# Routed experts of a GNN and MoE stack: visiting each expert once, in one of twelve ways by its count of rows

## The chip, the cores and the metric

The kernel runs on one core of one Trainium2 chip. The metric is device microseconds of one execution. The profile is a recording of one execution by the hardware profiler, and its span is the time from the first to the last recorded instruction.

## The reference

The state `x` has 625 rows (nodes) of 512 float32 features. Four layers follow each other, and each adds a graph part and then a feed-forward part to `x`, both of them on a layer norm of it. Layers 0 and 2 have feed-forward parts with eight small experts that see every row. The change concerns layers 1 and 3, where each row goes to two of eight large experts:

```python
# layer 1: 512 -> 1024 -> 512
logits = x @ gate_w + gate_b                      # 625 x 8
topk_vals, topk_idx = top_k(logits, 2); w = softmax(topk_vals)
h = relu(x @ w1[e] + b1[e]);  y_e = h @ w2[e] + b2[e];  out = sum_e w_e * y_e
# layer 3: 512 -> 1536 -> 512
probs = softmax(x @ router_w.T); gates, idx = top_k(probs, 2); gates /= sum(gates)
h = silu(x @ w1[e].T) * (x @ wgate[e].T);  y_e = h @ w2[e].T;  out = sum_e gate_e * y_e
```

So 1250 pairs of row and expert are computed in each of the two layers. The reference's router, on its inputs, gives the eight experts these counts of rows: in layer 1 they are 96, 346, 175, 23, 54, 50, 350 and 156; in layer 3 they are 197, 240, 352, 99, 77, 43, 149 and 93.

## The kernel before

The kernel is one program for all layers. A scheduler puts each instruction on its engine's queue in the order of the source, as far as the data allow, and sets semaphores between the engines. All matmuls of the experts are float32, and each shows in the trace as two matmul instructions, each with its weight load.

Weights lie in HBM as chunks of 128 partitions by 2048 float32 (1024 KB): an expert of layer 1 has 4 chunks (2 up, 2 down), one of layer 3 has 9 (6 up in 3 pairs of `w1` and `wgate`, 3 down). `routed` keeps a ring of 11 chunks. `refill` issues the next load on SyncE's queue as soon as a chunk has been read.

`dispatch` (L514) turns the router's choice into blocks of B = 128 rows. It ranks the rows of each expert with small matmuls (`ps_rk`), works out how many blocks each expert has beyond its first, gives each pair a place in one of NB = 17 blocks, and builds with one-hot matmuls (`ps_id`) the row numbers `node` and the weights `gate` of every block. Blocks 0 to 7 are the first blocks of the eight experts. Blocks 8 to 16 are overflow blocks; `own` names the expert of each of them.

`routed` (L619) then computes block by block. For each block:

- `fetch(b)` gathers 128 rows from HBM (an indirect DMA that GpSimd issues), two blocks ahead.
- `enter(b)` (L671) turns them with four TensorE transposes (`ps_x`) and copies them to `xgT`.
- `ahead(b, c)` multiplies the rows with an up chunk (`ps_h`, L1170 in layer 1, L1335 in layer 3): the 128 rows are the stationary side, 512 columns of weights are moved.
- `turn(b, c)` (L685) turns the hidden values (`ps_t`).
- `back(b, c)` (L692) multiplies them with a down chunk (`ps_y`, L697) and, after the last chunk, scales by `gate` (VectorE, L703) and adds the rows into `sums` in HBM (an indirect DMA that GpSimd issues, L705).

The first eight blocks are one straight list of units. The overflow blocks stand one inside the other in conditional blocks:

```python
def overflow(i):
    if i < NO:
        with tc.If(n_over > i):
            run([(E + i, c) for c in range(nch)], i + 1 < NO)
            overflow(i + 1)
```

Every engine executes each of these branches itself (L730 in the profile). The counts need 14 blocks in layer 1 (six of them overflow) and 13 in layer 3 (five overflow); an expert's weights are loaded again for each of its blocks.

In layer 1, `expert_bias` (matmuls `ps_eb`) and `normalise` (25 steps on VectorE and one on ScalarE, for the adjacency matrix of layers 2 and 3) are run as `fill` between the units of the first blocks.

Of the kernel before, what the change touches and what calls it, by code (L numbers as in the profile page):

```python
# [20 lines left out]
NT = 5  # L21
# [20 lines left out]

B = 128
NB = 17
NO = NB - E
# [31 lines left out]
def _weights(i):  # L77
# [15 lines left out]
    for e in range(E):  # L93
        a, g = _chunks(i["L3_ffn_w1"][e].T), _chunks(i["L3_ffn_wgate"][e].T)
        for c in range(3):
            w += [a[c], g[c]]
        w += _chunks(i["L3_ffn_w2"][e].T)
# [55 lines left out]
def kernel(  # L153
# [360 lines left out]
    def dispatch(layer, o12, weight, w0, per):  # L514


        with tc.tile_pool(name=f"{layer}d", bufs=1) as dp:
# [4 lines left out]
            rank, tot = ps[:T, 0, :NT * E], ps[:, 1, :E]  # L522
            nc.tensor.matmul(rank, tri, mask.rearrange("p t e -> p (t e)"), start=True, stop=False,
# [6 lines left out]
            for s in range(NT):  # L530
                nc.tensor.matmul(tot, ones16, mask[:, s, :], start=(s == 0), stop=(s == NT - 1))
            gt = dp.tile([P, E, 4], F32, tag="gt", name="gt")
            nc.vector.tensor_tensor(gt, tot[:, :, None].to_broadcast([P, E, 4]),
                                    thr[:, None, :].to_broadcast([P, E, 4]), op=OP.is_gt)
            nov = dp.tile([P, E], F32, tag="nov", name="nov")
            nc.vector.tensor_reduce(nov, gt, axis=AX.X, op=OP.add)
            pm = dp.tile([P, E, E], F32, tag="pm", name="pm")
            nc.vector.tensor_mul(pm, before, nov[:, None, :].to_broadcast([P, E, E]))
            ovb = dp.tile([P, E], F32, tag="ovb", name="ovb")
            nc.vector.tensor_reduce(ovb, pm, axis=AX.X, op=OP.add)  # L540
            delta = dp.tile([P, E], F32, tag="delta", name="delta")
            nc.vector.scalar_tensor_tensor(delta, ovb, float(B), dconst, op0=OP.mult, op1=OP.add)
            rk = rank.rearrange("p (t e) -> p t e", e=E)
            sl = dp.tile([T, NT, E], F32, tag="sl", name="sl")
            nc.vector.scalar_tensor_tensor(sl, rk, float(B),
                                           delta[:T, None, :].to_broadcast([T, NT, E]),
                                           op0=OP.is_ge, op1=OP.mult)
            nc.vector.tensor_add(sl, sl, rk)
            nc.vector.tensor_add(sl, sl, e128[:T, None, :].to_broadcast([T, NT, E]))
# [13 lines left out]
            ohp = dp.tile([T, 2 * NT, B], BF16, tag="ohp", name="ohp")  # L563
# [3 lines left out]
            nums = dp.tile([T, 2 * NT, NB, 2], BF16, tag="nums", name="nums")  # L567
            num = number.rearrange("p c t i -> p (c t) i")
            for i in range(2):
                nc.vector.tensor_mul(nums[:, :, :, i], ohb, bcast(num[:, :, i], NB))  # L570
            ps = pstile("ps_id")
            for n in range(2 * NT):
                nc.vector.tensor_scalar(ohp[:, n, :], place[:T, :], at[:, 0, n:n + 1], None,
                                        op0=OP.is_equal)
                nc.tensor.matmul(ps[:, 0, :2 * NB], ohp[:, n, :],
                                 nums[:, n].rearrange("p b i -> p (b i)"), start=(n == 0),
                                 stop=(n == 2 * NT - 1))
            one = dp.tile([P, NB], F32, tag="one", name="one")
            nc.vector.tensor_reduce(one, ps[:, 0, :2 * NB].rearrange("p (b i) -> p b i", i=2),
                                    axis=AX.X, op=OP.add)  # L580
            free = dp.tile([P, NB], F32, tag="free", name="free")
            nc.vector.tensor_scalar(free, one, 0.0, spare, op0=OP.is_equal, op1=OP.mult)
            node = small.tile([P, NB], I32, tag="node", name="node")
            nc.vector.scalar_tensor_tensor(node, one, -1.0, free, op0=OP.add, op1=OP.add)

            nc.vector.tensor_add(ovb, ovb, nov)
            le = dp.tile([P, NO, E], F32, tag="le", name="le")
            nc.vector.tensor_tensor(le, ovb[:, None, :].to_broadcast([P, NO, E]),
                                    blk[:, :NO, None].to_broadcast([P, NO, E]), op=OP.is_le)
            own = dp.tile([P, NO], F32, tag="own", name="own")  # L590
            nc.vector.tensor_reduce(own, le, axis=AX.X, op=OP.add)
            nc.vector.tensor_scalar(own, own, float(E - 1), None, op0=OP.min)
            whose = small.tile([P, NO, E], F32, tag="whose", name="whose")
            nc.vector.tensor_tensor(whose, own[:, :, None].to_broadcast([P, NO, E]),
                                    eio[:, None, :].to_broadcast([P, NO, E]), op=OP.is_equal)
            routing[layer] = small.tile([1, NO + 1], I32, tag="own_i", name="own_i")
            nc.vector.tensor_scalar(routing[layer][:, :NO], own[0:1, :], float(per), float(w0),
                                    op0=OP.mult, op1=OP.add)
            nc.vector.tensor_copy(routing[layer][:, NO:], ovb[0:1, E - 1:])

            rest = dp.tile([T, 2 * NT], F32, tag="rest", name="rest")
            nc.vector.tensor_copy(rest, weight)
# [14 lines left out]
        return node, gate, whose  # L617

    def routed(layer, node, gate, nch, nw, hidden, turned, first_fill=(), fill=()):  # L619
# [3 lines left out]
        w0, per = (W_L1, 4) if layer == "L1" else (W_L3, 9)  # L623
        assert state["taken"] == state["loaded"] == state["stop"]
        with tc.tile_pool(name=f"{layer}w", bufs=1) as more, \
# [9 lines left out]
            slots = kpool.tile([P, NT, D], F32, tag="K", name="slots")  # L635
            xgs = [slots[:, n, :] for n in range(3)]
            ys_out = [slots[:, n, :] for n in range(3, 5)]
            xgTs = [rpool.tile([P, KD, B], F32, name=f"xgT{n}") for n in range(2)]
            brought = {"n": 0}
            read = set()  # L640
            first = {}
            hs, hTs, ys = {}, {}, {}

            def bring(n):

                b, j = divmod(n, per)
                if b < E:
                    load(ring[n % RING], weights[w0 + n])
                    return
                if b not in first:  # L650
                    first[b] = nc.sync.value_load(routing[layer][0:1, b - E:b - E + 1],
                                                  min_val=w0, max_val=w0 + per * (E - 1))
                src = weights[bass.ds(first[b] + j, 1)].rearrange("a p m -> (a p) m")
                nc.sync.dma_start(ring[n % RING].rearrange("p k m -> p (k m)"), src,
                                  cond=n_over > b - E)

            def refill():

                while brought["n"] < NB * per:
                    n = brought["n"]  # L660
                    if n >= RING and n - RING not in read:
                        return
                    bring(n)
                    brought["n"] += 1

            def fetch(b):
                nc.gpsimd.indirect_dma_start(
                    out=xgs[b % 3], out_offset=None, in_=rows_hbm,
                    in_offset=bass.IndirectOffsetOnAxis(ap=node[:, b:b + 1], axis=0))

            def enter(b):  # L671
                pt = pstile("ps_x")
                for k in range(KD):
                    nc.tensor.transpose(pt[:, 0, k * B:(k + 1) * B],
                                        xgs[b % 3][:, k * P:(k + 1) * P], ident)
                evac(xgTs[b % 2].rearrange("p k s -> p (k s)"), pt[:, 0, :])

            def ahead(b, c):
                n = b * per + c * nw
                hs[b, c] = hidden(pstile("ps_h"), pool, c, xgTs[b % 2],  # L680
                                  [ring[i % RING] for i in range(n, n + nw)])
                read.update(range(n, n + nw))
                refill()

            def turn(b, c):  # L685
                pt, h = pstile("ps_t"), hs.pop((b, c))
                for j in range(4):
                    nc.tensor.transpose(pt[:, 0, j * B:(j + 1) * B], h[:, j * P:(j + 1) * P], ident)  # L688
                hTs[b, c] = pool.tile([P, 4, B], F32, tag="hT", name="hT")
                turned(hTs[b, c], pt[:, 0, :].rearrange("p (j s) -> p j s", j=4), c, b, pool)  # L690

            def back(b, c):  # L692
                if c == 0:
                    ys[b] = pstile("ps_y")
                hT, n = hTs.pop((b, c)), b * per + nch * nw + c
                for j in range(4):
# [646 lines left out]
    def l3_turned(hT, pt, c, b, pool):  # L1343
        evac(hT, pt)
# [35 lines left out]
```

## Time and profile before

| | |
|---|---|
| times of three runs | 1723.18, 1723.20 and 1728.77 us; median 1723.2 us |
| the profiled execution | 1723.04 us, span 1721.1 us |
| TensorE busy | 1528.4 us (89% of the span) |
| VectorE, ScalarE, GpSimd busy | 676.1, 357.8, 235.5 us |
| mean granted TensorE clock | 0.936 |
| layer 1, routed blocks | about 794 to 1018 us |
| layer 3, routed blocks | about 1282 to 1709 us |
| 1024 KB loads of expert weights through the ring | 195 issued |

"Busy" is the time in which an engine had at least one instruction running; matmuls overlap, so the mean duration of one is longer than its share of the busy time. "128x512" behind a tile is partitions by elements. An arrow gives outputs and inputs by the program's names.

### The profile page before, as it was taken

The numbers are of one execution on the slowest core, as the hardware profiler recorded it, in microseconds if no ns is written. First come the engines' busy times: TensorE is split into PE (matmuls) and PEld (weight loads), VectorE is DVE, ScalarE is ACT, GpSimd is POOL, SyncE is SP. The second block draws the span as 40 slices with busy tenths as digits, with TensorE's granted clock in tenths as the row PEclk, the third lists the DMA queues.
The fourth block names the chain that finished last, engine by engine and source line by source line (L and its number), as shares of the span: only waits on it lengthen the run. The fifth ranks groups of instructions, "written<-read, shape, count | busy, mean of one in ns | idle before, by whom it ended". The sixth has DMA issues, their size and how long they took to land.

```text
span 1721.1 us, 15559 instructions
## 1 busy us (share of the span) xinstructions
PE 1528.4 (89%) x5642; PEld 861.3 (50%) x5642; DVE 676.1 (39%) x1738; ACT 357.8 (21%) x680; POOL 235.5 (14%) x254
## 2 busy tenths in 40 slices
PE   7996999989897989846999969698759999999997
PEld 5774466555555656533444436354534444444443
DVE  9824562451974168466122225635331111111110
ACT  1102362011661046311111115301211000000100
POOL 2010042010540034101111112001000000000000
PEclk8998999999999989977999989799869999999998
DMA  3000200011001100136889731011258888869871
GB/s 135 16 28 25 73 1 25 31 68 53 22 1 49 49 26 1 40 112 234 302 270 342 256 87 73 25 49 49 102 217 299 301 309 304 307 244 359 311 265 50
DMA packets 40142, 237.12 MB, mean 138 GB/s; under 512 B 4779, under 2 KB 4907, under 8 KB 14299
## 3 DMA queue, kind: packets, MB, share of 16 engines
q1 hardware_dynamic: 30705, 214.80, 33.7%
q0 software_dynamic: 6608, 15.99, 4.1%
q10 hardware_dynamic: 2746, 5.25, 1.0%
q8 instruction: 48, 0.79, 0.2%
q14 instruction: 35, 0.29, 0.1%
HBM read 246.11 MB, written 14.26 MB: 151 GB/s over the span
## 4 chain that ended last, share of the span: by engine, by line
PE 70%; DVE 12%; issue 10%; DMA 4%; ACT 2%; POOL 1%; SPq 0%; POOLq 0%; ACTq 0%; DVEq 0%
PE ps_mf L359 17%; PE ps_y L697 9%; PE ps_h L1335 9%; PE ps_mn L367 7%; PE ps_h L1170 5%; PE ps_s L796 4%; PE ps_eo L496 4%; PE ps_o L860 3%; DMA sumsL<-slots,node 3%; PE ps_p L839 3%; PE ps_tr L328 2%; DVE ln_st L277 1%; DVE s L802 1%; PE ps_t L688 1%; DVE dst L913 1%
## 5 line engine op out<-in xcount | busy, mean ns | idle before, releaser
L1335 PE MATMUL ps_h<-ring,xgT 128*128 128x512 f32 x624 | 274.8, 595 | 0.8 <-DVE xgT L226 0.8
L697 PE MATMUL ps_y<-ring,hT 128*128 128x512 f32 x536 | 239.2, 593 | 0.9 <-issue 0.9
L1335 PEld LDWEIGHTS ps_h<-ring,xgT 128*128 128x128 f32 x624 | 118.7, 191 | 147.9 <-issue 145.3
L697 PEld LDWEIGHTS ps_y<-ring,hT 128*128 128x128 f32 x536 | 97.6, 190 | 103.9 <-issue 103.0
L825 POOL TENSOR_SCALAR s<-s,rs 125x625 f32<-125x625 f32 (+4 forms) x120 | 103.2, 875 | 294.0 <-DVE rs L822 269.9
L705 POOL DMA_INDIRECT sumsL<-slots,node x27 | 42.6, 1578 | 469.3 <-DVE slots L703 358.6
L1338 ACT ACTIVATE g<-ps_h 128x512 f32<-128x512 f32 x39 | 23.3, 597 | 395.6 <-PE ps_h L1335 364.5
L1170 PE MATMUL ps_h<-ring,xgT 128*128 128x512 f32 x224 | 103.2, 609 | 2.1 <-ACT xgT L234 1.3
L807 ACT ACTIVATE s<-s,mn 125x626 f32<-125x626 f32 (+4 forms) x120 | 87.2, 743 | 49.3 <-DVE mn L802 49.1
L802 DVE CUSTOM_DVE_ANT_0 s<-ps_s,mask 125x626 f32<-125x626 f32 (+4 forms) x120 | 82.6, 718 | 29.0 <-PE ps_s L796 27.8
L796 PE MATMUL ps_s<-kT,qT 64*125 64x313 f32 (+4 forms) x416 | 86.4, 466 | 2.8 <-DVE mn L802 2.8
L328 PE MATMUL ps_tr<-ident,xn 125*128 125x125 f32 x140 | 30.2, 398 | 62.6 <-DVE ln_nb L300 49.1
L226 DVE COPY hT<-ps_t 128x512 f32<-128x512 f32 x26 | 18.0, 692 | 171.5 <-PE ps_t L688 171.5
L1340 DVE TENSOR_TENSOR h<-ps_h,g 128x512 f32<-128x512 f32 x39 | 26.8, 686 | 147.9 <-ACT g L1338 147.9
L839 PE MATMUL ps_p<-ident,s 125*125 125x125 f32 x432 | 65.8, 293 | 14.0 <-POOL s L825 11.7
L359 PE MATMUL ps_mf<-xT,w 128*128 128x313 f32 x256 | 69.7, 434 | 6.6 <-ACT xT L402 6.6
L839 PEld LDWEIGHTS ps_p<-ident,s 125*125 125x125 f32 x432 | 53.9, 194 | 40.0 <-POOL s L825 28.6
L1170 PEld LDWEIGHTS ps_h<-ring,xgT 128*128 128x128 f32 x224 | 43.6, 196 | 57.5 <-issue 53.8
L817 DVE SCALAR_TENSOR_TENSOR s<-s,cnt 125x626 f32<-125x626 f32 x80 | 67.3, 863 | 9.9 <-ACT s L807 9.9
L496 PE MATMUL ps_eo<-w,h 128*125 128x512 f32 x160 | 70.6, 592 | 0.0
L860 PE MATMUL ps_o<-pT,v 125*64 125x375 f32 (+2 forms) x448 | 60.1, 413 | 9.0 <-DVE mn L802 4.2
L916 PE MATMUL ps_a<-dst,src 125*128 125x313 f16 x400 | 58.0, 309 | 6.9 <-DVE dst L913 5.3
(345 smaller groups left out, 1994.8 us busy)
## 6 DMA issues: line engine op xcount, KB each, us to landing
ring<-in_weights SPq DMA_DIRECT2D x195, 1024.0 KB
w<-in_weights SPq DMA_DIRECT2D x27, 1024.0 KB
rows_hbm<-xn ACTq DMA_DIRECT2D x2, 1120.0 KB
sumsL<-x ACTq DMA_DIRECT2D x2, 1120.0 KB
out<-sumsL SPq DMA_DIRECT2D x1, 1250.0 KB
x<-in_x SPq DMA_DIRECT2D x1, 1120.0 KB
x<-sumsL SPq DMA_DIRECT2D x5, 224.0 KB
rows<-in_rows SPq DMA_DIRECT2D x1, 1052.0 KB
```

The source lines that it names most:

```text
L359: nc.tensor.matmul(ps[:, half, :HC], w, r[:, half * HC:(half + 1) * HC], start=(n == 0), stop=(n == last))
L367: nc.tensor.matmul(ps[:T, 0, :width], src[:, k, t * T:(t + 1) * T], w[:, k, :width], start=(k == 0), stop=(k == KD - 1 and extra is None))
L496: nc.tensor.matmul(ps[:T, 0, :], h[:, t * T:(t + 1) * T], w, start=(f == 0), stop=(f == len(blocks) - 1))
L697: nc.tensor.matmul(ys[b][:, 0, :], hT[:, j, :], ring[n % RING][:, j, :], start=(c == 0 and j == 0), stop=(c == nch - 1 and j == 3))
L796: nc.tensor.matmul(ps[hh][:T, i, :w], qT[rr, b, t * T:(t + 1) * T], kT[rr, b, i * w:(i + 1) * w], start=True, stop=True)
L802: nc.vector.tensor_tensor_reduce(s[:, hh, :nb * w].rearrange("p (a c) -> p a c", a=nb), ps[hh][:T, :nb, :w], mask[:, t, :nb * w].rearrange ...
L807: nc.scalar.activation(s[:, hh, :nb * w], s[:, hh, :nb * w], AF.Exp, bias=mn[:, hh:hh + 1], scale=-1.0, accum_out=sm[:, hh:hh + 1] if caus ...
L825: nc.gpsimd.tensor_scalar(s[:, hh, :w], s[:, hh, :w], rs[:, hh:hh + 1], 1.0, op0=OP.mult, op1=OP.mult)
L839: nc.tensor.transpose(pp[:T, hh, j * T:(j + 1) * T], s[:, hh, j * T:(j + 1) * T], ident[:T, :T])
L860: nc.tensor.matmul(po[rr, 0, o:n * T], v[:, j, h * DH:(h + 1) * DH], pT[:, hh, j, o:n * T], start=(j == 0), stop=(j == nk - 1))
L1170: nc.tensor.matmul(ps[:, 0, :], xgT[:, k, :], w1[:, k, :], start=(k == 0), stop=(k == KD - 1))
L1335: nc.tensor.matmul(ps[:, i, :], xgT[:, k, :], w[i][:, k, :], start=(k == 0), stop=(k == KD - 1))
```

## The change

`dispatch` gives each expert five blocks of its own (NL = 5, NB = 40 columns in `node` and `gate`), whatever its count, so the overflow arithmetic goes (`gt`, `nov`, `pm`, `ovb`, `delta`, `le`, `own`, `whose`). The eight counts are read into registers of every engine. A second pair of tables, `node2` and `gate2`, addresses half blocks. Layer 3 ranks by the router's logits, without the softmax ahead of it. The bias term of layer 1 is computed inside `dispatch`, and `normalise` moves to the projections of the second graph step of layer 1.

`routed` visits each expert once. Its count picks one of twelve bodies through a binary tree of conditional blocks (`one_of`, `either`):

- up to 64 rows, a half block: 64 rows stationary, and each matmul of 512 columns is split into two of 256 columns, whose results go to partitions 0 to 63 and 64 to 127;
- up to 128, a block as before; up to 192, a block and a half block;
- up to 224, 256, 288, 320, 352, 384, 448 or 512, `wide`: the weights are the stationary side, and that many rows are moved; the hidden values come out already turned; the down matmuls go by blocks of 128 rows as before;
- above 512, `wide` and one more block.

Rows of the next expert are gathered one visit ahead, those beyond the first 128 in a nested condition (`fetch_more`). Each expert's weights are loaded once. The tree stands in the program eight times for each layer, one body after the other, the larger counts first.

```diff
-NB = 17
-NO = NB - E
+NL = 5
+NB = E * NL
+BH = B // 2
+WIDE = (224, 256, 288, 320, 352, 384, 448, 512)
...
-            w += [a[c], g[c]]
-        w += _chunks(i["L3_ffn_w2"][e].T)
+        w += [a[0], g[0], a[1], g[1], d[0], a[2], g[2], d[1], d[2]]
...
-            xgs = [slots[:, n, :] for n in range(3)]
+            xg_first = [rows_a[:, n, :] for n in range(3)]
+            xg_more = [rows_b[:, n, :] for n in range(NL - 1)]
+            _, counts = nc.values_load_multi_w_load_instructions(routing[layer][0:1, :],
+                                                                 min_val=0, max_val=N)
...
+            def fetch_more(e):
+                if e < E:
+                    with tc.If(counts[e] > B):
+                        gather(xg_more[0], node, e, 1)
+                        with tc.If(counts[e] > 3 * BH):
+                            for l in range(2, 4):
+                                gather(xg_more[l - 1], node, e, l)
...
+            class Block:                     # ahead, turn, back; in a half block:
+                    n = 2 if half else 1
+                    self.parts = [(slice(g * B // n, (g + 1) * B // n),
+                                   slice(g * 512 // n, (g + 1) * 512 // n)) for g in range(n)]
+                            for rr, cc in self.parts:
+                                nc.tensor.matmul(ps[rr, i, :n], self.xT[:, k, self.parts[0][0]],
+                                                 w[:, k, cc], start=(k == 0), stop=(k == KD - 1))
...
+            def wide(e, n, last):
+                nb = -(-n // B)
+                rows = [min(B, n - l * B) for l in range(nb)]
+                for l in range(nb):
+                    turned(xg_more[l - 1] if l else xg_first[e % 3], xwT[:, :, l * B:(l + 1) * B])
+                fetch_more(e + 1)
...
+                            nc.tensor.matmul(ps[:, i, :n], w[:, k, j * P:(j + 1) * P],
+                                             xwT[:, k, :n], start=(k == 0),
+                                             stop=(k == KD - 1))
...
+                    for l in range(nb):
+                        nc.tensor.matmul(ys[l // 2][:rows[l], l % 2, :],
+                                         hT[u][:, l * B:l * B + rows[l]],
+                                         chunk_of(e, down[c])[:, j, :], start=(u == 0),
+                                         stop=(u == 4 * nch - 1))
...
+            def either(e, above, yes, no):
...
+                with tc.If(counts[e] > above) as choice:
+                    yes()
...
+                with choice.Else():
+                    no()
...
+            ways = [(BH, lambda e: block(e, True)), (B, lambda e: block(e, False)),
+                    (B + BH, block_and_half)]
+            ways += [(n, lambda e, n=n: wide(e, n, True)) for n in WIDE] + [(N, all_of)]
+            def one_of(e, ways):
+                if len(ways) == 1:
+                    ways[0][1](e)
+                    return
+                i = len(ways) // 2
+                either(e, ways[i - 1][0], lambda: one_of(e, ways[i:]), lambda: one_of(e, ways[:i]))
+            for e in range(E):
+                one_of(e, ways)
```

## The prediction

> **What bounds the kernel now.** I read the page's head first (span, busy shares of the engines, packets by queue, shares of the chain of waits).
>
> ```profile
> span 1721.1 us, 15559 instructions
> PE 1528.4 (89%) x5642; PEld 861.3 (50%) x5642; DVE 676.1 (39%) x1738; ACT 357.8 (21%) x680; POOL 235.5 (14%) x254
> q8 instruction: 48, 0.79, 0.2%
> PE 70%; DVE 12%; issue 10%; DMA 4%; ACT 2%; POOL 1%; SPq 0%; POOLq 0%; ACTq 0%; DVEq 0%
> ```
>
> TensorE (PE) is the engine, but 89% is an average. So the routed stages next, as two windows: the overflow blocks of layer 1, and the end of layer 3. The columns are the window, its length, the busy time of PE, PEld, DVE, ACT, POOL, SP, the granted clock, the DMA share and GB/s.
>
> ```profile
> 926.00:1018.10 92.10, 91.08 (x263) 43.47 (x261) 20.87 (x64) 13.16 (x33) 15.50 (x12) 1.00 0.63 217
> 1526.70:1708.50 181.80, 181.72 (x492) 84.88 (x490) 23.35 (x35) 15.45 (x27) 14.48 (x11) 1.00 0.75 270
> ```
>
> TensorE is busy in 91.08 of 92.10 and in 181.72 of 181.80 us, at full clock, although a weight chunk is loaded for every block. So in both stages a microsecond off TensorE comes off the end, and a pause put in adds to it. Idle time ahead of the big groups confirms it, 0.8 and 0.9 us in all:
>
> ```profile
> L1335 PE MATMUL ps_h<-ring,xgT 128*128 128x512 f32 x624 | 274.8, 595 | 0.8 <-DVE xgT L226 0.8
> L697 PE MATMUL ps_y<-ring,hT 128*128 128x512 f32 x536 | 239.2, 593 | 0.9 <-issue 0.9
> ```
>
> Prices come from the chain (start, length) and the timeline:
>
> ```profile
> 708.34 17.07 PE ps_mf L359 x64
> 850.24 3.43 PE ps_h L1170 x8
> 1282.15 15.50 PE ps_h L1335 x32
> 1305.83 3.44 PE ps_y L697 x8
> ```
>
> ```profile
> 624.01 1.20 PE L839 MATMUL ps_p<-ident,s 125*125 125x125 f32 x4 [3.89 <-POOL s L825]
> 633.95 1.14 PE L839 MATMUL ps_p<-ident,s 125*125 125x125 f32 x8
> 649.19 2.33 PE L860 MATMUL ps_o<-pT,v 125*64 125x250 f32 x20 [0.70 <-DVE mn L802]
> ```
>
> An instruction that moves 512 columns is 3.44/8 = 0.43 us; one of 313 is 17.07/64 = 0.267, so 0.85 ns a column: 0.191 for 224, 0.218 for 256, 0.300 for 352. A block lasts 15.05 us in layer 1 (835.19 to 850.24; an overflow block 92.7/6 = 15.45) and 32.65 in layer 3 (same chunk of two neighbouring blocks, 1305.83 to 1338.48). Four transposes take 0.44.
>
> Last, the branches, since the change puts a tree of them ahead of every expert. L730 in three stretches: the run, the exit of layer 1, the exit of layer 3 (count: shortest/median/longest ns).
>
> ```profile
> L730 PEldq COMPARE_BRANCH  x15: 65/65/3839, 920.3 to 1708.6; - x15
> L730 PEldq COMPARE_BRANCH  x2: 187/270/352, 1012.3 to 1018.2; - x2
> L730 PEldq COMPARE_BRANCH  x2: 184/2012/3839, 1702.3 to 1708.6; - x2
> ```
>
> Falling through costs 65 ns. The exit of layer 1 skips three unused bodies, some 290 TensorE instructions, for 0.35 us at most. The exit of layer 3 skips four, some 740, and took 3.84 us. The array hid it: the branch began at 1702.3, the array ended at 1708.45, so the sequencer runs some 6 us ahead, 14 instructions of 0.43.
>
> **Part 1: less matmul work.** Counts are those of the reference.
> - *Wide.* An up chunk becomes 32 instructions of n columns, a down chunk 8 of 512 per 128 rows, and 0.44 of turning per 128 rows. Layer 3: 197 rows go as 224: 6 x 32 x 0.191 + 3 x 16 x 0.43 + 0.9 = 58.2 against 65.3 for two blocks; 240 as 256: 63.4 against 65.3; 352: 89.8 against 98.0. Layer 1 (2 up, 2 down): 346 and 350 go as 352, 2 x 32 x 0.300 + 2 x 24 x 0.43 + 1.3 = 41.1 against 45.95, twice. Sum -7.1 - 1.9 - 8.2 - 9.7 = -26.9.
> - *Half.* A chunk becomes 16 instructions of 256 columns, two to each former one, on 64 columns of the array. Nearest row: L860, also 64 wide, 20 instructions of 250 columns in 2.33, 0.117 each, so a pair runs side by side: 0.119 at 256, 1.9 us a chunk. From the other side, without overlap, 0.218 and 3.49 a chunk: nothing gained. I take the row of equal shape. Half block: 4 x 1.9 + 0.9 = 8.5 (layer 1), 9 x 1.9 + 1.1 = 18.2 (layer 3). Layer 1: 23, 54, 50 save 6.55 each, 175 and 156 (second block halved) 6.95 each, together -33.6; layer 3: 43 and 149 save 14.4 each, -28.8. Unpaired, these 62 us are lost.
> - 96, 99, 77 and 93 rows stay blocks: 0.
>
> Subtotal -89.3.
>
> **Part 2: what is moved.** Wide rows are turned inside their body and wait for the copy out, about 0.9 each (the transposes of two more groups), five times: +4.5. `ps_eb`, 2.0 and 2.8 us between units, moves into `dispatch` beside VectorE's ranking, about 1.5 of it ahead of the first turning: -3. Layer 3 loses its softmax from the path (1259.92 to 1261.35, 1.4) and 1.1 of short ranking steps; tables of 40 columns for 17 eat the same gain in layer 1: -2.5. Sum -1; bounds +10 and -10. Part 1 and 2: -90.
>
> Taken at nothing: `normalise` among the projections at 570 to 614 us, where VectorE is busy 3.5 of 31 us and its steps sum to about 13 (up to +13 without that cover). The counts' register loads, some 0.4 us on each engine, lie under the gathers (up to +3 each). 104 chunk loads for 195: the ring caused 1.6 us of idling; but a 43-row expert now eats 9 chunks in 18 us, which at the 270 GB/s of the window take 35 (the ring of 11 is full ahead; up to +13). SyncE's queue carries those loads alone and now passes the branches too; GpSimd's scatters queue behind each other, below.
>
> **Part 3: the jumps.** Every engine takes the whole tree. By the built order, TensorE's code grows from 12,567 to some 84,000 instructions; one tree of layer 3 alone holds thousands. On the counts above TensorE takes far jumps (348 instructions or more; 7 of them up to 515, the rest beyond): layer 1, ahead of the eight experts 2, 1, 3, 3, 3, 3, 1, 3; layer 3, 2, 3, 3, 4, 3, 3, 2, 4: 43 in all. Three transitions of layer 1 (first, second, seventh) have one more jump near 272 that I put at 2.0, between 0.35 and 3.84. A far jump is bounded by 0.35 (exit of 290) and 3.84 (exit of 740); most skip more than 740, so I take 3.84. Each follows on the last, so only the first is covered by the run-ahead: 6 us after a block or wide, 3 after a half (14 instructions of 0.218), 1.4 at a stage's start.
> - Layer 1: 2 x 3.84 + 2 - 1.4 = 8.3; 0; 11.5 - 6 = 5.5; 11.5 - 3 = 8.5 three times; 3.84 + 2 - 3 = 2.8; 5.5. Sum 47.6.
> - Layer 3: 6.3; 5.5; 5.5; 15.4 - 6 = 9.4; 5.5; 5.5; 7.7 - 3 = 4.7; 15.4 - 3 = 12.4. Sum 54.8.
> - Restart: after the 3.89 us pause at 624.01 four transposes took 1.20 where eight took 1.14, and layer 3's first 32 `ps_h` took 15.50 for 13.74, 1.8 more. Twelve of the pauses (five, seven) follow warm work: +22, with 0 and 12 x 4 as bounds.
>
> Sum +102 + 22 = +124.
>
> [...]
>
> **Sum.** The profiled execution is 1723.04 us (span 1721.1, 1.9 around it), the median 1723.2: no correction. 1723 - 90 + 124 = 1757.
>
> **The rivals.**
> *Jumps are cheap* (faster). If 3.84 was one odd fetch (the trace has one such jump), the 0.35 of the other exit holds, stalls vanish and the time is 1723 - 90 = 1633; at 2.0 us a jump the stalls are 25 and some restarts 7: 1665. It decides below 3.0 us, where stalls (68) and restarts (22) equal 90. For it: median 65 ns. Against: all of those were not taken or near. Chance 0.26.
> *A draw.* Jumps of 2.8 to 3.1 us, within 0.5% (8.6 us, about what a measurement of this kernel can tell from no change): 1723. Chance 0.06.
> *GpSimd becomes the bound.* A wide expert ends with two or three scatters, one behind the other, each 1.6 us of issue and, by the chain, 4.9 to 9.6 us to land; GpSimd also pays a semaphore step at a branch's end:
>
> ```profile
> L730 POOLq INC_SWDGE_SEM  x2: 858/1120/1383, 1019.5 to 1709.7; - x2
> ```
>
> The gather for the expert after next queues behind. Three scatters are 20 to 33 us against a next visit of 8.5 to 32; it decides once they outlast that visit. Five wide experts at some 6 us: 1757 + 30 = 1787. Against: the visits after wide ones last 23 us or more here. Chance 0.12.
> *Forecast*: jumps of 3.1 us and more, 1732 to 1810 (5 us a jump: stalls 152, restarts 25). Chance 0.56.
>
> **How the numbers follow.** Slower 0.56 + 0.12 = 0.68, same 0.06, faster 0.26. Jumps at 1640 and below hold about half of the cheap case (0.13); above 1820 lie unpaired halves and dearer jumps (0.07). So 1640 to 1820; the forecast's own range is 1732 to 1810.
>
> **What would show it.** TensorE's branch rows: some 40 of about 3.8 us, and idle gaps of 3 to 12 us ahead of each expert's first `ps_h` or `ps_x`, with slower matmuls behind. Half blocks: 16 `ps_h` in 1.9 us. Wide: 32 of 352 columns in 9.6 us. Loads 104. TensorE busy about 1440. Wrong if the far branches show under 3 us, or if the gaps end on ring loads or gathered rows.

## The result, and the profile after

| | before | after |
|---|---|---|
| median of the runs | 1723.6 us (4 runs, 1723.2 to 1728.8) | 1876.8 us (4 runs, 1875.1 to 1877.6) |
| ratio | 1 | 1.088, 95% interval 1.0858 to 1.0902 |
| span of the profiled execution | 1721.1 us | 1875.1 us |
| routed blocks of layer 1 (TensorE, first to last) | 226.2 us | 292.6 us |
| routed blocks of layer 3 | 428.1 us | 519.4 us |

The changed kernel is 8.8% slower. The forecast had the sign and the engine's jumps as the reason, but 1757 us: of the 153 us that the change costs it saw 34.

The head of the page after, with the same lines as before the change (the first two lines, the queue of instruction fetches, the chain's shares):

```profile
span 1875.1 us, 16516 instructions
PE 1485.8 (79%) x6074; PEld 905.8 (48%) x6074; DVE 654.2 (35%) x1663; ACT 346.3 (18%) x668; POOL 242.2 (13%) x260
q8 instruction: 140, 2.29, 0.6%
PE 62%; DVE 12%; DMA 9%; another core or an unknown queue 7%; issue 6%; ACT 2%; POOL 1%; POOLq 0%; SPq 0%; DVEq 0%; ACTq 0%
```

TensorE works 43 us less and the kernel lasts 154 us longer: its busy share fell from 89% to 79%. Instruction fetches on the queue q8 rose from 48 to 140. The chain's "another core or an unknown queue" is new: nearly all of it is four stretches of 20 to 51 us in layer 3 that the chain can't put down to anything of this core that the profile records. These stretches take in work of TensorE as well as pauses, so the pauses are read from the timeline and the branch rows below, not from the chain.

The two routed stages after, in the columns of the earlier windows (window, length, busy time of PE, PEld, DVE, ACT, POOL, granted clock, DMA share, GB/s):

```profile
797.80:1090.40 292.60, 193.54 (x752) 105.22 (x752) 32.73 (x72) 21.92 (x55) 36.59 (x31) 0.80 0.39 119
1342.20:1861.60 519.40, 400.80 (x1448) 238.46 (x1448) 46.51 (x86) 33.26 (x71) 34.61 (x29) 0.87 0.43 141
```

Before, TensorE was hardly idle in these stages, and the clock stood at 1.00 in both windows shown. Now it pauses for 99 of 292.6 us in layer 1 and for 119 of 519.4 in layer 3, at a mean granted clock of 0.80 and 0.87. VectorE and ScalarE are busy for less time than before, GpSimd for 242.2 us against 235.5, none of them near the span.

What a pause looks like in the timeline of TensorE, from the 352-row expert of layer 3 to the 99-row expert after it, and the branch rows of TensorE's queue in that stretch and in the whole run (count: shortest/median/longest ns):

```profile
1600.88 5.32 PE L871 MATMUL ps_y<-ring,hT 128*128 128x512 f32 x12
1622.78 15.57 PE L757 MATMUL ps_h<-ring,xbT 128*128 128x512 f32 x32 [16.58 <-issue]
```

```profile
L909 PEldq COMPARE_BRANCH  x5: 77/5058/6923, 1599.6 to 1616.8; - x5
```

```profile
L909 PEldq COMPARE_BRANCH  x71: 65/4560/8217, 800.6 to 1855.6; - x71
```

The array ends at 1606.2. Four of the five branches are far jumps (the fifth, of 77 ns, falls through); they last 22.3 us together, the last ends at 1622.2, and the first matmul follows 0.6 us later, "issue" being the profile's word for it. All sixteen transitions look like this one: the first matmul starts 0.2 to 1.2 us behind the last far jump, and these sixteen pauses make 207 of the 218 us. The 32 matmuls then take 15.57 us; after a pause of 0.47 us they take 13.97 (a row of the last kernel below). The same branches last 33 to 76 ns on the other four engines.

The new bodies themselves are as fast as worked out. The timeline, for an up chunk of a half block and a quarter of an up chunk of a wide one:

```profile
913.20 1.95 PE L757 MATMUL ps_h<-ring,xwT 128*64 128x256 f32 x16
855.46 2.53 PE L847 MATMUL ps_h<-xwT,ring 128*128 128x352 f32 x8
```

Sixteen instructions of 256 columns in 1.95 us (forecast 1.9), so the pairs do run side by side; eight of 352 columns in 2.4 from one to the next (8 x 0.300).

### The profile page after: what moved, and what is told of

It reads as the page before. It is cut to its first block, busy times and chain, and to the rows that moved or that the text cites. A ratio compares the mean times of both kernels' runs of the same rounds, so it can differ in the third digit from the quotient of the medians.

```text
span 1875.1 us, 16516 instructions
## 1 busy us (share of the span) xinstructions
PE 1485.8 (79%) x6074; PEld 905.8 (48%) x6074; DVE 654.2 (35%) x1663; ACT 346.3 (18%) x668; POOL 242.2 (13%) x260
## 3 DMA queue, kind: packets, MB, share of 16 engines
q8 instruction: 140, 2.29, 0.6%
## 4 chain that ended last, share of the span: by engine, by line
PE 62%; DVE 12%; DMA 9%; another core or an unknown queue 7%; issue 6%; ACT 2%; POOL 1%; POOLq 0%; SPq 0%; DVEq 0%; ACTq 0%
PE ps_mf L359 16%; PE ps_h L847 10%; PE ps_y L871 6%; PE ps_mn L367 6%; DMA sumsL<-rows_a,node 6%; PE ps_s L985 3%; PE ps_h L757 3%; PE ps_eo L496 3%; PE ps_o L1049 3%; PE ps_p L1028 3%; DMA rows_b<-rows_hbm,node 2%; PE ps_y L801 1%; PE ps_tr L328 1%; DVE ln_st L277 1%
## 5 line engine op out<-in xcount | busy, mean ns | idle before, releaser
L757 PE MATMUL ps_h<-ring,xbT 128*128 128x512 f32 (+1 forms) x432 | 152.3, 592 | 129.1 <-issue 129.1
L847 PE MATMUL ps_h<-xwT,ring 128*128 128x352 f32 (+2 forms) x704 | 188.3, 422 | 3.9 <-ACT xwT L234 2.2
L757 PEld LDWEIGHTS ps_h<-ring,xbT 128*128 128x128 f32 (+1 forms) x432 | 70.6, 202 | 205.3 <-issue 202.0
L847 PEld LDWEIGHTS ps_h<-xwT,ring 128*128 128x128 f32 x704 | 138.1, 197 | 61.6 <-issue 22.1
L735 POOL DMA_INDIRECT sumsL<-rows_a,node x27 | 42.1, 1561 | 644.5 <-DVE rows_a L734 553.7
L871 PE MATMUL ps_y<-ring,hT 128*128 128x512 f32 (+1 forms) x264 | 120.9, 592 | 0.0
L801 PE MATMUL ps_y<-ring,hT 128*64 128x256 f32 (+1 forms) x400 | 93.7, 458 | 1.2 <-ACT hT L789 1.2
L854 DVE TENSOR_TENSOR hT<-ps_h,g 128x224 f32<-128x224 f32 (+2 forms) x36 | 16.1, 447 | 184.2 <-ACT g L853 184.2
L1028 PE MATMUL ps_p<-ident,s 125*125 125x125 f32 x432 | 66.6, 296 | 13.7 <-POOL s L1014 10.9
L871 PEld LDWEIGHTS ps_y<-ring,hT 128*128 128x128 f32 (+1 forms) x264 | 47.4, 181 | 47.2 <-issue 41.9
L359 PEld LDWEIGHTS ps_mf<-xT,w 128*128 128x128 f32 x256 | 50.6, 199 | 27.5 <-ACT xT L402 7.1
```

The lines of the kernel that those rows point to most:

```text
L359: nc.tensor.matmul(ps[:, half, :HC], w, r[:, half * HC:(half + 1) * HC], start=(n == 0), stop=(n == last))
L757: nc.tensor.matmul(ps[rr, i, :n], self.xT[:, k, self.parts[0][0]], w[:, k, cc], start=(k == 0), stop=(k == KD - 1))
L801: nc.tensor.matmul(self.y[ro, 0, :n], hT[:, j, rr], w[:, g * nj + j, co], start=(c == 0 and g == 0 and j == 0), stop=(c == nch - 1 and g = ...
L847: nc.tensor.matmul(ps[:, i, :n], w[:, k, j * P:(j + 1) * P], xwT[:, k, :n], start=(k == 0), stop=(k == KD - 1))
L871: nc.tensor.matmul(ys[l // 2][:rows[l], l % 2, :], hT[u][:, l * B:l * B + rows[l]], chunk_of(e, down[c])[:, j, :], start=(u == 0), stop=(u ...
L1028: nc.tensor.transpose(pp[:T, hh, j * T:(j + 1) * T], s[:, hh, j * T:(j + 1) * T], ident[:T, :T])
```

## The experiments

The theory: TensorE's far jumps are the whole loss. What had to be settled was why it was twice as large as in the forecast (stalls of 211 us for 102). Beside the several experiments the kernel before measured 1723.6 to 1725.8 us, so a difference of some 2 us between two of them says nothing.

**Without the tree.** Each expert's body is picked while the program is built, from the reference's counts; such a kernel serves one input alone and is a measuring device.

```diff
-                i = len(ways) // 2
-                either(e, ways[i - 1][0], lambda: one_of(e, ways[i:]), lambda: one_of(e, ways[:i]))
+                [w for w in ways if KNOWN[layer][e] <= w[0]][0][1](e)
```

(and `fetch_more` with plain `if`s.)

> The changed kernel without its trees: each expert's body is built straight into the program, picked from the reference's counts, so the work is the same and no engine takes a branch. Theory (the jumps of TensorE are the whole loss): the 46 slow branch rows (252 us by their durations) and the pauses vanish, TensorE's routed stages run at full clock, and the time is 1723 - 90 = 1633 us (1625 to 1650). Rival (the bodies themselves gain less than worked out, or GpSimd's scatters hold them up): 1680 us or more even without branches.

Measured: 1627.9 us, ratio 0.943 (0.9411 to 0.945). The windows of its routed stages:

```profile
797.10:972.10 175.00, 172.65 (x752) 94.15 (x752) 31.88 (x71) 22.53 (x56) 35.70 (x32) 0.98 0.58 190
1225.30:1613.00 387.70, 383.14 (x1448) 229.79 (x1448) 45.55 (x85) 33.88 (x72) 34.37 (x29) 0.99 0.53 185
```

The same 752 and 1448 matmuls as in the changed kernel, 555.8 us of work for 594.3 and 6.9 us of pauses for 217.7. The difference of the two, 38.5 + 210.8 = 249.3 us, is the difference of the times (1876.8 - 1627.9 = 248.9). So parts 1 and 2 of the forecast hold, and all of the loss belongs to what the tree and its conditions bring: 211 us of pauses, and 38.5 us of slower matmuls (granted clock 0.80 and 0.87 for 0.98 and 0.99).

**Without reloading.** `while brought["n"] < E * per` becomes `< RING`, so after 11 chunks nothing is loaded and the DMA engines are quiet; the tree stays.

> The changed kernel with the tree, but only the first 11 weight chunks of each routed layer are loaded and then used again, so that the DMA engines are almost idle while TensorE jumps (the values are not the reference's). Theory A (instruction fetches share the DMA engines with the 1024 KB weight loads and wait behind them): the far branch rows fall from a mean of 5.5 us to 4.0 or less, the pauses by 60 us or more, and the time to 1810 us or less. Theory B (a jump waits for the fetch that the jump ahead of it has started, so jumps in a row are dear whatever the loads do): the mean stays at 5 us or more and the time within 20 us of 1877.

Measured: 1813.1 us. Layer 1's sums differ without those chunks, and with them layer 3's counts, so that only layer 1 compares row by row: 22 far jumps, on the mean 4.37 us for 4.99, pauses 83.0 for 99.1 us. Neither theory by its numbers: the loads' traffic has a part, not all.

**Quiet DMA engines in layer 3 alone**, with the counts kept: `< (RING if layer == "L3" else E * per)`.

> The changed kernel with layer 3 alone using its first 11 chunks again and again (its sums are not the reference's; layer 1 and the counts of layer 3 stay as they are), so the same 25 far jumps of layer 3 happen beside idle DMA engines. Theory A (the fetches wait behind weight loads): layer 3's far rows fall from 5.8 to about 4.7 us on the mean, its pauses from 118.6 to 85 to 95 us, the time to 1845 us or so. Rival: rows and pauses stay within 8%, and the time within 10 us of 1877.

Measured: 1849.5 us, pauses of layer 3 92.8 us for 118.6. The branch rows at the exit of the same 352-row expert as above (22.3 us for four):

```profile
L909 PEldq COMPARE_BRANCH  x5: 82/3463/6122, 1592.6 to 1607.7; - x5
```

Layer 3's 24 far jumps sum to 112.3 us, 4.68 each, for 141.6, 5.90 each (24 by the trace, the 25 of the expectation counted the layer's last exit). Theory A holds for this 1.2 us a jump.

The rest is seen when the rows are sorted. By their place: beside quiet DMA engines a jump that follows no other taken jump lasts 3.7 us on the mean (6 rows), close to the 3.84 from before; one that starts where another, far or near, has just landed lasts 5.0 (18 rows). The trace also records every packet of q8, the queue that the page calls "instruction" (2.29 MB in 140 packets in the changed kernel, 16.4 KB each); such a packet is called a fetch below. By the fetches that start in them the rows part more cleanly. Each far row holds one or two:

| layer 3, rows ahead of the experts | one fetch | two fetches |
|---|---|---|
| loads away | 6 rows, mean 3.38 us (2.96 to 3.60) | 18 rows, mean 5.11 us (4.64 to 6.12) |
| loads running (changed kernel) | 6 rows, mean 5.70 us (4.04 to 6.44) | 18 rows, mean 5.97 us (4.51 to 7.86) |

Without the loads the two kinds don't overlap. Place and number of fetches mostly go together in layer 3 (17 of the 18 rows in a row hold two), so layer 1 of the run before, also without loads, has to tell them apart. There sixteen jumps stand behind another: ten with two fetches last 5.06 us on the mean (4.60 to 5.86), six with one 3.64 (five of them 2.97 to 3.65, one 5.43). And when a jump of layer 3 begins here, no packet of the fetch queue is under way. So the wait for the fetch of the jump ahead, which theory B names, isn't in the trace: a jump in a row is dearer where it holds two fetches. What decides between one and two isn't shown.

**One and two far jumps**, put ahead of every expert of the kernel without the tree.

```diff
+            def jumps(e, k):
+                if k == 0:
+                    one_of(e, ways)
+                else:
+                    either(e, 600, lambda: wide(e, WIDE[-1], True), lambda: jumps(e, k - 1))
             for e in range(E):
-                one_of(e, ways)
+                jumps(e, 1)
```

> The kernel without the tree, with one far jump put ahead of every expert: a condition that never holds, over a dead body for 512 rows (over 1000 TensorE instructions). 16 single jumps, each behind a full queue of matmuls. Both theories: each jump shows as 4 to 6.5 us, mostly hidden by the 6 us that the sequencer runs ahead; halves hide 3. Time = the kernel without the tree + 10 to 30 us. If the sequencer's lead does not hide a jump: + 80 us or more.

Measured: 1702.4 us, + 74.5. The dead body is shorter than the expectation said, 303 to 306 instructions in layer 1 (295 for the last) and some 625 in layer 3. Of the 16 jumps 12 were far ones by their time, 4.0 to 6.9 us, and four of layer 1 took 0.33 at the same distance as four of these, so distance alone does not tell a far jump at that length. The packets of q8 do: each of the 12 long rows holds one, the four others none. The rise was far over the 10 to 30 us expected; the kernel with a plain condition, two experiments on, says why.

> The same with two far jumps in a row ahead of every expert. Theory B (jumps in a row wait for each other): the second row of each pair is at least 1.5 us longer than the first, and the time is that of the kernel with one jump + 16 x 7 + some 15 for restarts = + 125 us. Theory A (only the loads' traffic makes them dear): both rows of a pair alike at some 5.5 us, + 16 x 5.5 + 15 = + 105 us; a rise under 60 us would say that jumps overlap each other.

Measured: 1778.7 us, another 76.3; 28 far jumps. Neither number came. In layer 3, with loads running, first and second jumps of a pair last 5.75 and 6.16 us, not the 1.5 apart that B asked for; the changed kernel has 5.7 and 6.0.

**A condition without a jump.** The same kernel without the tree, with `with tc.If(counts[e] > 0):` around each body. It always holds and has no other branch.

> The kernel without the tree, with each expert's body inside a condition that always holds and has no other branch: every engine still compares and has a boundary ahead of each body, but nothing is skipped, so TensorE takes no jump. Theory (the far jumps are the loss): within 15 us of the 1628 us without the tree. Rival (the boundary itself costs, by semaphores, GpSimd's fix-ups and the lost overlap of neighbouring experts): of the 74.5 us that one jump per expert added, 40 or more are here, 1668 us or later.

Measured: 1670.8 us, + 42.9. Here the rival was right: of the 74.5 us for one jump, 43 come with a plain condition too, and 31.5 are left for the twelve far jumps (2.6 each that are not hidden). The trace of the kernel with one jump agrees: its pauses that overlap a far jump sum to 31 us. 34.5 of the 43 are in layer 1. The trace shows the largest piece, after the first 352-row body:

```profile
862.75 1.41 DVE L735 TENSOR_SCALAR rows_a<-ps_y,gate 128x512 f32<-128x512 f32 x2 [6.65 <-PE ps_y L872]
863.79 1.62 POOL L736 DMA_INDIRECT sumsL<-rows_a,node  x1 [37.91 <-DVE rows_a L735]
870.13 0.75 DVE L735 TENSOR_SCALAR rows_a<-ps_y,gate 96x512 f32<-96x512 f32 x1 [5.97 <-DMA sumsL<-rows_a,node]
870.80 0.68 DVE L227 COPY xwT<-ps_x 128x512 f32<-128x512 f32 x1
870.98 5.20 PE L758 MATMUL ps_h<-ring,xbT 128*128 128x512 f32 x6 [6.97 <-issue]
```

VectorE scales three blocks into two buffers; the third waits 5.97 us for the first scatter to land. Behind it on VectorE stands the next expert's copy of turned rows, and TensorE starts right after that copy, 6.97 us late. In the kernel without conditions the copy stands ahead of that third scaling, which waits for the scatter just as long and holds nothing up:

```profile
859.25 0.68 DVE L227 COPY xwT<-ps_x 128x512 f32<-128x512 f32 x1
865.31 0.75 DVE L735 TENSOR_SCALAR rows_a<-ps_y,gate 96x512 f32<-96x512 f32 x1 [5.38 <-DMA sumsL<-rows_a,node]
```

With a condition around each body the next expert's copy stays behind the scaling (870.80 after 870.13, where it stood at 859.25 ahead of 865.31).

**A third buffer** for the scaled sums, in the kernel with plain conditions:

```diff
+            y_out.append(rows_b[:, NL - 1, :])
-                y = y_out[flipy["n"] % 2][:ps.shape[0], :width]
+                y = y_out[flipy["n"] % 3][:ps.shape[0], :width]
```

> The kernel with a condition that always holds around each body (1670.8 us), with a third buffer for the scaled sums of the down matmuls. Theory (its 43 us over the kernel without conditions are mostly one mechanism: after a 352-row body the third scaling on VectorE waits some 6 us for the first scatter to land, and across the condition the next expert's copies of turned rows stand behind it): TensorE's pauses of 6.97 and 5.19 us after the two 352-row bodies of layer 1 shrink to under 2, and with the restarts the time falls by 12 to 18 us to 1653 to 1659. Rival (the pauses are the boundary itself): no change, within 4 us of 1671.

Measured: 1651.5 us, - 19.3, a little more than expected; both pauses are 0.91 us now. The group that stood at 870.13 is no longer late:

```profile
860.63 0.74 DVE L736 TENSOR_SCALAR rows_a<-ps_y,gate 96x512 f32<-96x512 f32 x1
861.29 0.68 DVE L227 COPY xwT<-ps_x 128x512 f32<-128x512 f32 x1
```

A pause of 5.4 us stays, for rows whose gather queues on GpSimd behind the scatter of a half block, which is the forecast's GpSimd rival in small.

The same third buffer in the changed kernel, and in the chain that follows:

> The changed kernel with its tree and a third buffer for the scaled sums, the edit that took 19 us off the kernel with plain conditions. Theory (in the changed kernel TensorE's jumps last as long as these waits or longer, and hide them): within 6 us of 1877. Rival (waits and jumps add up): 1862 us or less.

Measured: 1876.7 us, no change. TensorE's jumps last longer than those waits and hide them, so the 19 us that this edit took off the kernel with plain conditions can't be taken off the changed kernel. The rest of the 43 was not tried there.

**The tree as a chain**, `i = 1` for `i = len(ways) // 2`: the same bodies, at most two far jumps to each.

> The changed kernel with the same twelve bodies, but the tree as a chain: above 64? above 128? above 192? and so on, so that every body is reached with at most two far jumps. By the built order some 22 to 25 far jumps for 47. Theory (the loss goes by jumps, above all by jumps in a row): stalls of about 60 us for 211, restarts 30, boundaries 20, on the 1628 us without a tree: 1738 us (1715 to 1765). Rival (the loss goes by the size of the code or by the distance of a jump, which is up to 6135 instructions here for 3808): no better than 1850.

Measured: 1774.9 us, 102 less, with 23 far jumps for 46 ahead of the bodies; fetches of instructions 99 for 140. Half of the jumps gone took 41% of the loss (249 us) away, and the longer distances did no harm that shows: a far row lasts 5.20 us on the mean, for 5.47. It is 37 us dearer than expected: pauses 121 us, of which I had put 60 to the jumps and 20 to the boundaries. Ten of the pauses over 1 us end within 1.3 us of a far jump; they sum to 57 us, close to the 60 put to them. Eight end 4.8 to 6.8 us behind the last far jump and sum to 57 us as well. Two of these eight:

```profile
828.91 1.94 PE L717 MATMUL ps_x<-ident,rows_b 128*128 128x128 f32 x8 [5.18 <-DMA sumsL<-rows_a,node]
1660.55 1.09 PE L717 MATMUL ps_x<-ident,rows_b 128*128 128x128 f32 x4 [11.47 <-DMA sumsL<-rows_a,node]
```

So with half of the jumps gone, waits between neighbouring bodies come out that hardly show in the changed kernel; the 20 us for the boundaries was the term that was too small.

> The chain of conditions (1774.9 us) with the third buffer. Here layer 1 has pauses of 5.2, 9.0 and 6.4 us after or between jumps of 3.5 to 5.4 us; theory: the jumps hide part of the waits, 5 to 12 us are gained: 1763 to 1770 us. Rival as above: 1757 or less; or nothing, if the jumps alone set these pauses.

Measured: 1775.4 us, no change. The three pauses are 5.4, 7.7 and 5.9 us now, and they end 4.0 to 7.0 us behind the last far jump, by the profile on the landing of a scatter. So neither the jumps alone nor the lack of a buffer sets them; what would shorten them was not tried.

**Half blocks without far jumps.** What remains is to take the part of the change that pays most for the least code. Into the kernel before: a flag for each block says whether it has more than 64 rows, and an overflow block is run whole or half.

```diff
                     with tc.If(n_over > i):
-                        run([(E + i, c) for c in range(nch)], i + 1 < NO)
+                        either(E + i, i + 1 < NO)
                         overflow(i + 1)
+            def either(b, more_after):
...
+                with tc.If(big > 0) as choice:
+                    run(units, more_after)
...
+                with choice.Else():
+                    run(units, more_after, True)
```

> The kernel before, with one thing of the change: an overflow block of up to 64 rows is run as a half block (a condition inside each overflow block, block first, half block behind it); weights, blocks and dispatch as before. Saved: two halves in layer 1 (175 and 156 rows) 6.95 each, one in layer 3 (149) 14.4, together 28.3. Theory: in layer 1 no jump skips over 250 instructions, so each costs 0.3; in layer 3 four blocks end with one single far jump behind a full queue, hidden; boundaries 0.5 to 1.5 us for each of 11 blocks: 1723 - 28 + 10 = 1705 us (1695 to 1718). Rival (single jumps and boundaries cost 4 us each, as the kernel with one jump per expert showed on the mean): 1723 - 28 + 44 = 1739.

Measured: 1695.8 us, ratio 0.9828 (0.9814 to 0.9841), at the lower end of what was expected.

The second version does the same for experts 3 to 7 among the first blocks: `run` for three straight blocks, then `for b in range(3, E): either(b, True)`.

> The kernel before with half blocks for overflow blocks (1695.8 us) and for five of the first eight blocks too (experts 3 to 7; the first three stay straight code, so that the work between units has its place). Saved: 23, 54 and 50 rows in layer 1, 6.55 each, and 43 rows in layer 3, 14.4: 34.1. Against it: five more boundaries in each layer, 0.4 each in layer 1 for the lost overlap, and four more single jumps of 315 instructions in layer 3, hidden behind a full queue; after half blocks in layer 1 the exit jump is covered less. Theory: 1696 - 34 + 10 = 1672 us (1662 to 1682). Rival (in layer 1, bodies of 8.5 us are too short for the scatters and gathers on GpSimd, as the 5.3 us wait for gathered rows in the kernel with conditions showed): 1685 us or more.

Measured: 1666.1 us, ratio 0.9663 (0.9648 to 0.9678), as expected and the fastest kernel here that takes its counts from the router. In TensorE's timeline, a block's first 32 matmuls after a pause of 0.47 us, and a transition of layer 3 from a whole block to a half one:

```profile
1597.74 13.97 PE L1439 MATMUL ps_h<-ring,xgT 128*128 128x512 f32 x32 [0.47 <-issue]
1623.61 7.03 PE L766 MATMUL ps_y<-ring,hT 128*128 128x512 f32 x16
1631.46 1.95 PE L711 MATMUL ps_h<-ring,xgT 128*64 128x256 f32 x16 [0.83 <-issue]
1633.84 5.40 PE L711 MATMUL ps_h<-ring,xgT 128*64 128x256 f32 x48 [0.43 <-issue]
```

A pause of 0.83 us in place of the 9 to 19 of the changed kernel's layer 3. It has 8 far jumps in all, of 3.4 to 5.9 us, none behind another far one: the array's queue hides them, and the pauses of both stages sum to some 16 us.

## Why the forecast came out as it did

*What bounds the kernel*: right. With TensorE busy throughout, every pause went onto the end one for one, 249.3 us of pauses and slower work for 248.9 of time.

*Part 1 and 2, - 90 us*: right as a sum; the kernel without the tree measured - 95.7 against 1723.6 (- 97.4 against its own comparison runs). The row of L860 was the right one for the half blocks.

*The number of jumps, 46*: right; 46 far rows stand ahead of the sixteen experts. *The near jumps at 2.0 us*: wrong; the three of them lasted 3.06, 2.98 and 6.09.

*The price of a far jump, 3.84 us*: the step that failed. The 46 rows sum to 251.5 us, 5.47 each, where the forecast summed 171 (with its three near ones): + 80. The one row of before was a jump with one fetch (one packet of q8 lies in it), 29 us after the last weight load had landed, and it was right for that kind (3.4 to 3.8 on the mean). With the loads away the rows sum to 43 us less (13.7 in layer 1, 29.3 in layer 3); the three near jumps make 6; the other 31 or so belong to the jumps with two fetches, 29 of the 46, which are dearer beside quiet DMA engines too (5.11 us on the mean for 3.38 in layer 3). I had both bounds of the price from one recording, without loads beside the dear one, and treated the upper one as the end of the range; the 5 us that I tried as a worst case was below the mean.

*The cover*: 69 us forecast, 41 left by the measurement (251.5 - 211, a remainder that takes in all else). After wide bodies and whole blocks the array ran on for 4.7 to 6.6 us where 6 was foreseen, but after halves 1.7 to 2.3 for 3, at the start of layer 1 nothing, and the first matmul starts 0.2 to 1.2 us behind the last jump: + 28.

*The restarts*: 22 us forecast, 38.5 measured. The clock went lower than a single short pause had shown: 0.80 and 0.87 as means of the stages, and 1.6 to 2.7 us more for the first 16 matmuls of layer 1's blocks and the first 32 of layer 3's, where 1.8 was foreseen (9.49 for 7.03, 16.70 for 13.97). + 16.

Together - 6 + 80 + 28 + 16 = 118 of the 120 us between forecast and result.

*The rivals.* Cheap jumps and a draw fell. GpSimd as the bound was there as a mechanism, at two places (the landing of the first scatter, worth 19 us, and a gather behind a scatter), in the kernel with plain conditions, and such waits come out in the chain; in the changed kernel the jumps hide the first, and a third buffer gains nothing there. The conditions themselves stood nowhere in the sum; in the changed kernel some 10 us of the 218 us of pauses lie outside the sixteen transitions.

In each of the 47 far rows of the changed kernel (46 and the last exit) one or two packets of q8 start: one in 18 rows, the exit among them, and two in 29.

## What to carry to other kernels

On an engine that bounds the kernel, price a condition by the taken jumps that reach its body, not by its compares: in layer 3 here 77 ns for the branch that fell through behind the 352-row expert, 3.4 us on the mean for a far jump with one fetch beside quiet DMA engines, 5.1 for one with two, 5.7 and 6.0 beside weight loads, and at most 6.6 us of all that stood in a row were hidden by the queue. Keep to one far jump between two bodies: two ways, half and whole block, that brought 59 of the 96 us beat twelve ways that would have brought them all. Measure the bodies first without their conditions: one run told gain and loss apart, and a condition that always holds then showed what the boundary alone costs.

## What the runs showed of the hardware that was not expected

The price of a far jump went with the number of fetches in its row and with what the DMA engines did: in layer 3 it was 3.38 us on the mean with one fetch and 5.11 with two when the weight loads of the layer were taken away, 5.70 and 5.97 with them. Four jumps over 303 to 306 instructions took 0.33 us and four of nearly the same length 4.1 to 5.0 us in one run, while 246, 272 and 273 instructions took 3.0 to 6.1 us in another (lengths by the built order): the distance alone did not tell near from far. In the first run each of the long rows holds a fetch and the short ones none; what makes a jump fetch was not settled. And pauses of 3.5 to 17.7 us between bodies left TensorE at a mean granted clock of 0.80 over layer 1's routed blocks, in which the same matmuls took 193.5 us for 172.7 at 0.98.
